# Layer 1's input stage: the silu of a strip moved into the next strip's convolution, and its normalised input made one strip earlier

## The chip, the cores and the metric

The kernel runs on one core of a Trainium2 chip, in float32. The time is the device time of one execution in microseconds (us), from three runs. A core has engines that run side by side and in order, each through its own queue: TensorE (PE; its weight loads are listed as PEld), VectorE (DVE), ScalarE (ACT), GpSimd (POOL), and SyncE (SP), which here only issues DMAs. An engine that waits for a semaphore holds everything behind it in its queue.

## The reference

A batch of 8 images of 64 x 64 pixels with 192 channels goes through four layers, each of the form x + f(group norm of x). Layer 0 is a state-space block with convolutions and an MLP, layers 2 and 3 are 3 x 3 depthwise convolutions. The change lies in layer 1, a two-dimensional selective scan, and there in what comes ahead of the scan:

```
xz = einsum("bhwc,oc->bhwo", gn(x), in_proj_w)       # 192 -> 768
xa, z = split(xz, 2)                                 # 384 each
xc = depthwise_conv3x3(xa, conv_w) + conv_b
xc = silu(xc)
x_dbl = einsum("bkdl,kcd->bkcl", xs(xc), x_proj_weight)   # 4 directions, 44 rows each
...                                                  # scan over 4096 positions in 4 directions
```

`z` is made later, in the output stage of the layer.

## The kernel before

The program runs five stages one after the other: layer 0, the input stage of layer 1 (`layer1_in`), its scan, its output stage, and layers 2 and 3 together. The stages hand over through DRAM: `x1` comes from layer 0; `ur` (the silu's result, channels on partitions), `ut` (the same, positions on partitions) and `xd` (the projection for the scan) go to the scan.

`layer1_in` works in 64 strips: 8 images of 8 strips, a strip being 8 image rows, that is 512 positions (`NJ`). The 384 channels are 3 groups of 128 (index `o`). Three Python generators emit the instructions, and `together` takes a step of each in turn, in the order `turn`, `convolve`, `project`; a `yield` ends a step. The engines' queues hold exactly this order, as it is written out by hand (`every_engine`). A generator that has to wait yields until a count in `done` allows it to go on.

- `project` (L783 to L802), for strip q: `normed` (L734) issues the DMA of `xt` on SP and two ACT instructions (L739) that make the group-normed `g`. For each `o`, PE makes two matmuls `mm` (L793), and ACT copies the result into `xa` (L797), which has room for one image row above and one below. POOL then fills these border rows from the neighbouring strip (L799, L800).
- `convolve` (L804 to L835), for strip q: for each `o`, PE does the three vertical taps of the middle column as matmuls with diagonal matrices (`cv`, L815), ACT takes them out of PSUM with the bias (L817), and DVE adds the other six taps one by one (L823). After the third `o` one ACT instruction does silu on the whole of `u` (L832), and `done["conv"]` goes up. Because of the border row, convolution of strip q needs the projection of strip q+1; the projection emitted beside it is that of q+2.
- `turn` (L837 to L861), for strip q: SP sends `u` to `ur` (L843). For each of 4 blocks of 128 positions PE transposes `u` (three transposes, `tp`, L849) and projects it (three matmuls, `xp`, L852); I call this a pair. ACT copies the transposes into `uT` (L856), DVE copies the projections into `xdt` (L857). Then SP sends both away (L858, L859). `turn` begins when `done["conv"]` is at least q+2, so it is two strips behind the one being convolved.

The pools rotate: `u` and `xa` have four buffers, `xt`, `g` and `uT` two, and every PSUM tag (`mm`, `cv`, `tp`, `xp`) two banks.

The matmuls are float32. The trace lists each of them as two entries where 512 columns are moved, so an `mm` group (two matmuls) is four entries and a `cv` group (three) is six.

Of the kernel before, what the change touches and what calls it, by code (L numbers as in the profile page):

```python
# [10 lines left out]
AF = mybir.ActivationFunctionType  # L11
# [22 lines left out]
def mk(pool, shape, tag, **kw):  # L34
    Names.n += 1
    return pool.tile(shape, F32, tag=tag, name=f"{tag}_{Names.n}", **kw)
# [44 lines left out]
def make_diag(nc, pool, w, nct, ident, tag, plus_one=False):  # L81
    P = w.shape[0]
    dg = mk(pool, [P, nct, 3, P], tag)
    for ct in range(nct):
        for j in range(3):
            s = w[:, ct, 3 * j + 1 : 3 * j + 2]
            if j == 1 and plus_one:
                nc.vector.scalar_tensor_tensor(dg[:, ct, j, :], ident[:P, :P], s, ident[:P, :P], ALU.mult, ALU.add)
            else:
                nc.vector.tensor_scalar(dg[:, ct, j, :], ident[:P, :P], s, None, ALU.mult)  # L90
    return dg
# [55 lines left out]
def together(*threads, beside=()):  # L147

    threads = list(threads)
    while threads:  # L150
        for t in list(threads) + list(beside):
            if next(t, threads) is threads and t in threads:
                threads.remove(t)


def every_engine(tc):
    ET = mybir.EngineType
    return tc.manual_schedule(engines={ET.PE, ET.DVE, ET.Activation, ET.Pool})
# [595 lines left out]
@with_exitstack  # L754
def layer1_in(ctx: ExitStack, tc, a, load, w_in, normed, ur, ut, xd, cst):

    nc = tc.nc
    ident = cst[0]
    wp = ctx.enter_context(tc.tile_pool(name="wi1", bufs=1))
    cw, cb = load("conv_w", [DP, DT, 9]), load("conv_b", [DP, DT])  # L760
    w_xp = load("w_xp", [DP, DT, K1 * XC])
    dg = make_diag(nc, wp, cw, DT, ident, "dg")
    sb = ctx.enter_context(tc.tile_pool(name="si1", bufs=2))
    psum = ctx.enter_context(tc.tile_pool(name="pi1", bufs=2, space=PSUM))
    xdt = [mk(wp, [128, NJ // 128, K1, 1 + XC], f"xdt{i}") for i in range(2)]
    for t in xdt:
        nc.vector.memset(t, 1.0)
    R = NJ // W
    strips = [(b, r) for b in range(B) for r in range(NCH)]
    rows, us = {}, {}  # L770
    done = {"in": 0, "conv": 0, "out": 0}

    def xa_rows(q):

        if q not in rows:
            t = rows[q] = mk(sb, [DP, DT, (R + 2) * W], "xa", bufs=4)
            if strips[q][1] == 0:
                nc.gpsimd.memset(t[:, :, 0:W], 0.0)
            if strips[q][1] == NCH - 1:
                nc.gpsimd.memset(t[:, :, (R + 1) * W :], 0.0)  # L780
        return rows[q]

    def project():  # L783
        for q, (b, r) in enumerate(strips):
            while done["conv"] < q - 2:
                yield
            _, g = normed(sb, b, r)
            yield
            t = xa_rows(q)
            for o in range(DT):  # L790
                ps = mk(psum, [128, NJ], "mm")
                for ct in range(CT):
                    nc.tensor.matmul(  # L793
                        ps, w_in[:, ct, o * 128 : (o + 1) * 128], g[:, ct, :], start=ct == 0, stop=ct == CT - 1
                    )
                yield
                nc.scalar.copy(t[:, o, W : W + NJ], ps)  # L797
            if r > 0:
                nc.gpsimd.tensor_copy(t[:, :, 0:W], rows[q - 1][:, :, NJ : NJ + W])  # L799
                nc.gpsimd.tensor_copy(rows[q - 1][:, :, NJ + W :], t[:, :, W : 2 * W])  # L800
            done["in"] = q + 1
            yield  # L802

    def convolve():  # L804
        for q, (b, r) in enumerate(strips):
            while done["in"] < q + 1 + (r < NCH - 1) or done["out"] < q - 2:
                yield
            t = rows[q]
            u = us[q] = mk(sb, [DP, DT, NJ], "u", bufs=4)
            uv = u.rearrange("p d (h w) -> p d h w", w=W)  # L810
            tv = t.rearrange("p d (h w) -> p d h w", w=W)
            for o in range(DT):
                ps = mk(psum, [128, NJ], "cv")
                for dy in range(3):
                    nc.tensor.matmul(ps, dg[:, o, dy, :], t[:, o, dy * W : dy * W + NJ], start=dy == 0, stop=dy == 2)  # L815
                yield
                nc.scalar.activation(u[:, o, :], ps, AF.Identity, bias=cb[:, o : o + 1])  # L817
                yield
                for dy in range(3):
                    for dx in (-1, 1):  # L820
                        w0, w1 = max(0, -dx), W - max(0, dx)
                        tap = 3 * dy + dx + 1
                        nc.vector.scalar_tensor_tensor(  # L823
                            uv[:, o, :, w0:w1],
                            tv[:, o, dy : dy + R, w0 + dx : w1 + dx],
                            cw[:, o, tap : tap + 1],
                            uv[:, o, :, w0:w1],
                            ALU.mult,
                            ALU.add,
                        )  # L830
            yield
            nc.scalar.activation(u, u, AF.Silu)  # L832
            del rows[q]
            done["conv"] = q + 1
            yield  # L835

    def turn():  # L837
        for q, (b, r) in enumerate(strips):
            while done["conv"] < min(q + 2, len(strips)):
                yield  # L840
            u = us.pop(q)
            t0 = r * NJ
            nc.sync.dma_start(ur[b][:, :, t0 : t0 + NJ], u)  # L843
            uT = mk(sb, [128, NJ // 128, DIN], "uT")
            xt = xdt[q % 2]
            for i in range(NJ // 128):
                ps = mk(psum, [128, NJ], "tp")
                for o in range(DT):
                    nc.tensor.transpose(ps[:, o * 128 : (o + 1) * 128], u[:, o, i * 128 : (i + 1) * 128], ident)  # L849
                px = mk(psum, [128, NJ], "xp")  # L850
                for o in range(DT):
                    nc.tensor.matmul(  # L852
                        px[:, 0 : K1 * XC], u[:, o, i * 128 : (i + 1) * 128], w_xp[:, o, :], start=o == 0, stop=o == 2
                    )
                yield
                nc.scalar.copy(uT[:, i, :], ps[:, 0:DIN])  # L856
                nc.vector.tensor_copy(xt[:, i, :, 1:], px[:, 0 : K1 * XC].rearrange("p (k c) -> p k c", k=K1))  # L857
            nc.sync.dma_start(ut[b][t0 : t0 + NJ, :].rearrange("(t q) d -> q t d", q=128), uT)  # L858
            nc.sync.dma_start(xd[b][t0 : t0 + NJ].rearrange("(t q) k c -> q t k c", q=128), xt)  # L859
            done["out"] = q + 1  # L860
            yield  # L861

    with every_engine(tc):
        together(turn(), convolve(), project())
# [447 lines left out]
```

## Time and profile before

| | us |
|---|---|
| median of 3 runs | 26510.6 |
| lowest and highest run | 26507.2, 26526.69 |
| the profiled execution | 26508.04 |
| its span, first to last instruction | 26506.2 |
| layer 0 | 0 to about 5745 |
| input stage of layer 1 | about 5745 to 7435 |
| scan of layer 1 | about 7435 to 23690 |
| output stage of layer 1 | about 23690 to 24960 |
| layers 2 and 3 | about 24960 to 26506 |

The scan takes 16255 of the 26506 us; of it nothing is touched. The stage in question has 1690 us, 6.4% of the span. The mean granted TensorE clock over the whole run is 0.942 of full speed; in the input stage it is 0.87, in the scan 1.00.

How a line is read: a group's line names the line of the kernel, the engine, the operation and the tiles (written <- read), then the total busy time, the mean duration of one in ns, and after the second bar the idle time of the engine just ahead of these instructions with what ended it. In a timeline, the first number is the start in us from the span's start, the second the duration; the bracket is the idle time before and what ended it. A line of stretches gives for each engine the busy time, with the number of instructions in brackets, in the order PE, PEld, DVE, ACT, POOL, then the granted clock, the DMA engines' share and GB/s. Ends of matmuls are modelled, so lengths on PE are best taken from start to start.

### The profile page before, as it was taken

How to read it: one execution, taken by the hardware profiler on the slowest of the kernel's cores; microseconds unless marked ns; L12 is line 12 of the kernel's file. 1: busy time of each engine (PE TensorE's matmuls, PEld its weight loads, DVE VectorE, ACT ScalarE, POOL GpSimd, SP SyncE). 2: the span in 40 equal slices, each digit the busy share in tenths (PEclk: the TensorE clock that was granted, in tenths of full speed). 3: DMA queues.
4: the chain of work that ended last, by engine and by line, in shares of the span. 5: the costliest groups of instructions: out<-in, count | busy, mean ns of one | idle time of the engine just before them, and what ended most of it. 6: DMA issues, size and time to landing. Idle time of an engine off the chain costs nothing.

```text
span 26506.2 us, 442347 instructions
## 1 busy us (share of the span) xinstructions
PE 23817.3 (90%) x156160; PEld 18514.6 (70%) x156160; DVE 22196.4 (84%) x25001; ACT 20110.0 (76%) x40019; POOL 17618.6 (66%) x18396
## 2 busy tenths in 40 slices
PE   7888888887799999999999999999999999987766
PEld 4444444444478888888888888888888888863322
DVE  6777777655589999999999999999999999986566
ACT  4555555433379999999999999999999999984322
POOL 2222222210079999999999999999999999972100
PEclk8888888888899999999999999999999999998878
DMA  1111111112233333333333333333333333346411
GB/s 55 42 43 43 42 43 42 34 44 89 90 103 97 94 102 96 95 101 96 96 100 98 94 101 97 96 99 98 95 99 99 95 98 97 96 137 198 126 34 29
DMA packets 1461962, 2275.55 MB, mean 86 GB/s; under 512 B 247181, under 2 KB 773133, under 8 KB 1458202
## 3 DMA queue, kind: packets, MB, share of 16 engines
q1 hardware_dynamic: 1445402, 2196.90, 28.2%
q0 software_dynamic: 14336, 50.34, 0.5%
q8 instruction: 1232, 20.19, 0.3%
q14 instruction: 992, 8.13, 0.1%
HBM read 1811.37 MB, written 435.42 MB: 85 GB/s over the span
## 4 chain that ended last, share of the span: by engine, by line
PE 36%; ACT 29%; DVE 13%; POOL 13%; issue 6%; DMA 2%; POOLq 0%; SPq 0%; DVEq 0%; ACTq 0%
ACT dA L1039 12%; POOL hc L1089 10%; PE pd L1045 6%; ACT sb L1023 6%; PE yt L978 5%; DVE h L1080 5%; ACT bd L1023 4%; PE y L643 3%; PE fc L677 3%; DVE x L71 2%; DVE u L823 2%; PE mm L793 2%; DMA yin<-y 2%; PE pd L1047 2%; PE mm L399 2%
## 5 line engine op out<-in xcount | busy, mean ns | idle before, releaser
L1089 POOL TENSOR_TENSOR hc<-h,bc 128x512 f32<-128x512 f32 x12288 | 15425.9, 1289 | 488.7 <-DVE h L1080 342.0
L1080 DVE TENSOR_TENSOR_SCAN h<-dA,st,pd 128x512 f32<-128x512 f32 x10752 | 12949.9, 1263 | 530.9 <-PE pd L1045 369.4
L1039 ACT ACTIVATE dA<-dl,A_logs 128x512 f32<-128x512 f32 x12288 | 8787.0, 715 | 46.9 <-DVE h L1080 39.6
L978 PE MATMUL yt<-sq,hc 128*128 128x128 f32 x49152 | 7488.5, 275 | 198.8 <-POOL hc L1089 97.3
L1045 PE MATMUL pd<-bd,dut 128*128 128x128 f32 x49152 | 6582.1, 277 | 254.4 <-DVE h L1080 232.1
L1045 PEld LDWEIGHTS pd<-bd,dut 128*128 128x128 f32 x49152 | 5969.2, 192 | 610.3 <-PE yt L978 343.0
L978 PEld LDWEIGHTS yt<-sq,hc 128*128 128x128 f32 x49152 | 5668.1, 141 | 642.1 <-POOL hc L1089 623.3
L1023 ACT ACTIVATE sb<-dut,xt 128x384 f32<-128x384 f32 x8192 | 4763.5, 606 | 1.1 <-DVE dut L964 1.0
L1047 PE MATMUL pd<-sq,sb 128*128 128x128 f32 x24576 | 3739.5, 275 | 9.1 <-DVE h L1080 0.2
L1047 PEld LDWEIGHTS pd<-sq,sb 128*128 128x128 f32 x24576 | 2820.9, 141 | 480.6 <-DVE dl L951 380.8
L1023 ACT ACTIVATE bd<-sq,xt 128x128 f32<-128x128 f32 x8192 | 3011.1, 393 | 0.0
L1080 DVE TENSOR_TENSOR_SCAN h<-dA,pd 128x512 f32<-128x512 f32 x1536 | 1772.6, 1204 | 114.8 <-PE pd L1045 75.6
L71 DVE SCALAR_TENSOR_TENSOR x<-x,w,x 96x3969 f32<-96x3969 f32 (+1 forms) x192 | 838.3, 4366 | 488.6 <-ACT x L64 485.6
L538 POOL TENSOR_TENSOR xdt<-xb,dtv 128x384 f32<-128x384 f32 x256 | 220.7, 862 | 1365.5 <-ACT xb L532 1365.5
L800 POOL COPY xa<-xa 128x192 f32<-128x192 f32 x56 | 19.9, 356 | 1387.9 <-ACT xa L797 1387.9
L413 POOL COPY halo<-raw 128x12 f32<-128x12 f32 x64 | 12.8, 201 | 1380.8 <-ACT raw L403 1380.8
L304 DVE SCALAR_TENSOR_TENSOR x<-xs,cpe_w,x 96x504 f32<-96x504 f32 (+1 forms) x1024 | 899.4, 878 | 30.2 <-ACT x L292 20.4
L823 DVE SCALAR_TENSOR_TENSOR u<-xa,conv_w,u 128x504 f32<-128x504 f32 x1152 | 850.1, 743 | 63.5 <-ACT u L817 25.1
L937 PE MATMUL mm<-xs,w_dt 13*128 13x512 f32 x1536 | 863.0, 641 | 1.8 <-DVE dl L951 1.0
L677 PE MATMUL fc<-ff,fc_w 128*96 128x512 f32 x1536 | 858.9, 676 | 2.7 <-DVE xo L680 2.7
L1091 POOL COPY st<-h 128x3 f32<-128x3 f32 x4096 | 821.8, 201 | 0.0
L793 PE MATMUL mm<-g,w_in 96*128 96x512 f32 x768 | 487.5, 769 | 333.4 <-ACT g L739 332.9
(234 smaller groups left out, 26955.9 us busy)
## 6 DMA issues: line engine op xcount, KB each, us to landing
bc<-bcd SPq DMA_DIRECT2D x4096, 256.0 KB
yin<-y SPq DMA_DIRECT2D x256, 768.0 KB
csb<-csd SPq DMA_DIRECT2D x256, 384.0 KB
dut<-ut SPq DMA_DIRECT2D x128, 768.0 KB
y<-ys SPq DMA_DIRECT2D x128, 768.0 KB
dut<-ut SPq DMA_DIRECT2D x256, 384.0 KB
y<-ys SPq DMA_DIRECT2D x256, 384.0 KB
xt<-x1d SPq DMA_DIRECT2D x128, 384.0 KB
```

Of the source, the lines that this page charges most:

```text
L71: nc.vector.scalar_tensor_tensor(d[:, h0:h1, w0:w1], s[:, h0 + dy : h1 + dy, w0 + dx : w1 + dx], w[:, ct, tap : tap + 1], d[:, h0:h1, w0:w ...
L304: nc.vector.scalar_tensor_tensor(d[:, :, w0:w1], s[:, dy : dy + R, w0 + dx : w1 + dx], w[:, ct, tap : tap + 1], d[:, :, w0:w1], ALU.mult, ...
L677: nc.tensor.matmul(ps, f2w[:, o, ct * CP : (ct + 1) * CP], ff[:, o, :], start=o == 0, stop=o == 5)
L793: nc.tensor.matmul(ps, w_in[:, ct, o * 128 : (o + 1) * 128], g[:, ct, :], start=ct == 0, stop=ct == CT - 1)
L823: nc.vector.scalar_tensor_tensor(uv[:, o, :, w0:w1], tv[:, o, dy : dy + R, w0 + dx : w1 + dx], cw[:, o, tap : tap + 1], uv[:, o, :, w0:w1] ...
L978: nc.tensor.matmul(yt[:, t * 128 : (t + 1) * 128], src[:, t * 128 : (t + 1) * 128], mat, is_transpose=mat is ident, start=first and t == 0 ...
L1023: nc.scalar.activation(v, src, AF.Copy, scale=m["xt"][:, t, 1 + R1 + n : 2 + R1 + n])
L1039: nc.scalar.activation(dA, ready[s]["dl"][:, o, :], AF.Exp, scale=aneg[:, k, o, n : n + 1])
L1045: nc.tensor.matmul(dst, ready[s]["dut"][:, t, cols], brows[g, t], start=True, stop=True)
L1047: nc.tensor.transpose(dst, brows[g, t][:, cols], ident)
L1080: nc.vector.tensor_tensor_scan(h[:, o, rev], decay.pop(j)[:, rev], turned.pop(j)[:, rev], 0.0 if first else st[:, o, n : n + 1], ALU.mult, ...
L1089: nc.gpsimd.tensor_tensor(hc, h[:, o, :], held[g], ALU.mult)
```

## The change

```diff
     def project():
+        _, g = normed(sb, *strips[0])
         for q, (b, r) in enumerate(strips):
             while done["conv"] < q - 2:
                 yield
-            _, g = normed(sb, b, r)
-            yield
             t = xa_rows(q)
             for o in range(DT):
                 ps = mk(psum, [128, NJ], "mm")
...
                 yield
                 nc.scalar.copy(t[:, o, W : W + NJ], ps)
+            if q + 1 < len(strips):
+                _, g = normed(sb, *strips[q + 1])
             if r > 0:
...
                 yield
                 nc.scalar.activation(u[:, o, :], ps, AF.Identity, bias=cb[:, o : o + 1])
+                if o == 0 and q > 0:
+                    finish(q - 1)
                 yield
...
             yield
-            nc.scalar.activation(u, u, AF.Silu)
-            del rows[q]
-            done["conv"] = q + 1
-            yield
+        finish(len(strips) - 1)
+        yield
+
+    def finish(q):
+        nc.scalar.activation(us[q], us[q], AF.Silu)
+        del rows[q]
+        done["conv"] = q + 1
 
     def turn():
         for q, (b, r) in enumerate(strips):
-            while done["conv"] < min(q + 2, len(strips)):
+            while done["conv"] < q + 1:
                 yield
```

The silu of a strip is no longer issued at the end of its own convolution. `finish` issues it in the next strip's convolution, behind the first of that strip's three copies out of PSUM. `normed` for a strip is called at the end of the projection of the strip before, behind the third copy into `xa`, so its DMA and its two ACT instructions are emitted earlier; the step that it took for itself is gone. `turn` begins when its strip's silu is issued. The arithmetic, the tiles, the buffers and the number of instructions stay the same.

## The prediction

> **What bounds the kernel now.** I read the totals of the page first, then the stretches of the stages, then, inside the stretch of the input stage of layer 1, the groups, the waits, one strip of the timeline and the granted clock.
>
> ```profile
> PE 23817.3 (90%) x156160; PEld 18514.6 (70%) x156160; DVE 22196.4 (84%) x25001; ACT 20110.0 (76%) x40019; POOL 17618.6 (66%) x18396
> ...
> 5745.00:7435.00 1690.00, 1332.90 (x4247) 758.51 (x4246) 925.19 (x1479) 528.20 (x841) 40.74 (x128) 0.87 0.26 89
> ```
>
> The totals say little: they are an average over five stages. The second line is the stretch of the input stage (columns: length, then busy time of PE, PEld, DVE, ACT, POOL, granted clock, DMA share, GB/s): 1690 us, in which DVE works 925, ACT 528, and the DMA engines are busy 26%. PE shows 1333, but partly at a lowered clock. No engine is full, so the stage is a chain of waits. Its largest groups and waits:
>
> ```profile
> L823 DVE SCALAR_TENSOR_TENSOR u<-xa,conv_w,u 128x504 f32<-128x504 f32 x1152 | 850.1, 743 | 63.5 <-ACT u L817 25.1 <-DVE u L823 0.9
> ...
> L832 ACT ACTIVATE u<-u 128x1536 f32<-128x1536 f32 x64 | 94.9, 1482 | 394.0 <-DVE u L823 387.5 <-DVE xdt L857 6.5
> L857 DVE COPY xdt<-xp 128x176 f32<-128x176 f32 x256 | 86.3, 338 | 689.6 <-PE xp L852 689.6
> ...
> DVE xdt L857 <- PE xp L852: 689.6, 128, 8.3
> ACT u L832 <- DVE u L823: 387.5, 62, 6.3
> ...
> PE mm L793 <- ACT g L739: 332.9, 62, 6.4
> ```
>
> They form a ring: silu (L832) waits 6.3 us per strip for DVE's taps, PE waits 5.4 us for `g` (L739), which ACT issues behind that silu, and DVE waits for PE's projection `xp`. One strip shows it in order:
>
> ```profile
> 6414.68 1.48 ACT L832 ACTIVATE u<-u 128x1536 f32<-128x1536 f32 x1 [6.27 <-DVE u L823]
> 6416.07 1.50 ACT L739 ACTIVATE g<-xt,nbb,scb 96x512 f32<-96x512 f32 x2
> ...
> 6416.92 3.78 PE L793 MATMUL mm<-g,w_in 96*128 96x512 f32 x4 [5.44 <-ACT g L739]
> ...
> 6423.14 0.34 DVE L857 COPY xdt<-xp 128x176 f32<-128x176 f32 x1 [8.30 <-PE xp L852]
> ...
> 6428.74 1.88 PE L793 MATMUL mm<-g,w_in 96*128 96x512 f32 x4
> ...
> 6432.15 9.18 DVE L823 SCALAR_TENSOR_TENSOR u<-xa,conv_w,u 128x504 f32<-128x504 f32 x12
> ...
> 6441.42 1.48 ACT L832 ACTIVATE u<-u 128x1536 f32<-128x1536 f32 x1 [6.27 <-DVE u L823]
> ```
>
> From one silu to the next are 26.74 us here. From the first silu (5791.13) to the 62nd (7383.42), the last before two strips that have no more input projection, are 61 steps in 1592.3 us, 26.10 on average. The same four `mm` take 3.78 us after PE's pause and 1.88 later: the clock.
>
> ```profile
> 6436.90:6440.40 3.50, 1.32 (x4) 0.26 (x2) 3.36 (x5) 0.00 (x0) 0.00 (x0) 1.00 0.00 0
> 6440.40:6447.30 6.90, 3.64 (x5) 1.47 (x6) 1.14 (x3) 3.84 (x5) 0.00 (x0) 0.52 0.45 151
> 6447.30:6463.70 16.40, 16.27 (x63) 9.54 (x61) 11.19 (x18) 4.28 (x8) 0.64 (x2) 1.00 0.23 79
> 24640.93:24643.41 2.48, 0.45 (x1) 0.24 (x2) 1.76 (x1) 0.59 (x2) 2.06 (x1) 1.00 0.37 123
> 24643.88:24647.30 3.42, 3.42 (x5) 1.11 (x4) 1.07 (x1) 0.64 (x1) 2.31 (x1) 0.50 0.01 3
> 24469.14:24471.62 2.48, 0.06 (x1) 0.06 (x1) 1.76 (x1) 0.57 (x1) 0.00 (x0) 1.00 1.07 364
> 24471.62:24475.10 3.48, 3.48 (x9) 1.35 (x10) 0.00 (x0) 1.52 (x2) 3.19 (x1) 1.00 0.12 28
> ```
>
> The last column but two is the granted clock. A pause of 5.4 us halves it for 6.9 us. Pauses of 2.48 us, in the output stage, did it once (24643.88: 0.50) and not the other time (24471.62: 1.00). The trace's clock records change only at multiples of 3.41 us. Laying the pauses of about 2 to 4 us against that grid: with 1.98 us or more of pause inside one cell a full clock was always lowered for the next cell, with less the 2.48 us pauses never lowered it.
>
> [...] The trace has one such load (1283 ns) for 64 silus among Identity and Copy, so silu's new neighbours, of the same two kinds, cost no load.
>
> **The change part by part.** Per strip nothing is added or removed: 3 convolution groups, 3 input projections, 4 pairs of transpose and `xp`, 18 taps, 4 `xdt` copies, and the same DMAs. The orders change. Call the strip in convolution q. On PE, up to a rotation: cv0(q), mm0(q+2), pair 0 of q-1, cv1, mm1, pair 1, mm2, pair 2, cv2, pair 3. On ACT: cv0's copy, silu of q-1, the copies and transposes' copies, `g` of q+3 after the third `xa` copy. On DVE: taps 0, two `xdt` copies, taps 1, two copies, taps 2, and at once taps 0 of the next strip. `turn` now follows one strip behind, not two.
>
> *The waits removed.* `g` is made a strip ahead, so mm0 no longer waits for it: the 5.4 us of PE. Taps 0 of the next strip no longer stand behind `xp`: they run 4.6 us while silu runs.
>
> *The wait added.* Pair 0 of q-1 now needs silu of q-1, which needs taps 2. Behind that pair in PE's order stand cv1, mm1 and the rest of the strip, and DVE's second and fourth `xdt` copies wait for pairs 1 and 3. This makes the new ring. At full clock, from starts in the timeline: a convolution group 2.57 us (6426.17 to 6428.74), an `mm` group 1.72 (to 6430.46), a pair 1.23 (to 6431.69). The ring is
> silu 1.48; 0.15 to the first transpose (0.10 is seen from `g` to the weight load, 0.05 is my estimate); three pairs 3.69, cv1 and cv2 5.14, mm1 and mm2 3.44, and the fourth pair to its end 1.39 (6430.46 to 6431.85), together 13.66; 0.04 and 0.26 for `xdt`; six taps 4.59 (half of 9.18); 0.09 to silu. Sum 20.27 us.
> Beside it: pair 1 ends 8.5 us after silu's start, its copy and taps 1 end near 13.4, before pair 3 (15.3), so that branch has 1.6 us to spare. PE's own work is 3 x 2.57 + 3 x 1.72 + 4 x 1.23 = 17.79, DVE's 18 x 0.765 + 4 x 0.3 = 15, ACT's 8.7. So PE pauses 20.27 - 17.79 = 2.48 us in each strip, before pair 0.
>
> *The clock.* This pause lies just where the trace has both outcomes. By the grid, a pause of 2.48 lowers the clock when 1.98 us fall in one cell: 1.93 of 3.41 positions. A lowered cell costs half of 3.41, 1.7 us, on the ring. But the positions are not drawn at random: six cells are 20.48 us, so a strip of 20.27 moves the pause 0.21 earlier against the grid each time, until it enters the bad part, is delayed by up to 1.7 us, and leaves it again. The mean then settles at 20.48 (one lowered strip in eight). The kernel before does the same: its strips repeat 25.38, 26.32, 26.81, which are 23 cells. Bounds: never lowered 20.27, always lowered 21.97. I take 20.48.
>
> *Costed at nothing.* `xt` for `g` of q+3 is issued by SP behind the `ur` transfer, which waits for silu: about 2.3 us into the ring. In the trace both had landed 3.6 us after the issue of `xt` (6444.34 to about 6448), and ACT wants it only at about 10.8; cv2's copy behind it may be 2 us later still. Were it late, each us past that would be on the ring. The `ut` and `xd` transfers follow as before. `u` has four buffers, `xa` four, so one more strip held by silu frees them late by a copy only. POOL's halo copies (0.35 us) come after the third `xa` copy, about 4 us ahead of cv0 of the next strip.
>
> *Edges.* The last two strips without `mm`: 20.27 - 3.44 = 16.8, plus 1.7 for a pause of over 4 us, 18.5 each, against 18.41 and 18.09: +0.5. The tail holds four pairs after the last silu, not six: -2.5. In the beginning mm1 stands ahead of cv1: +0.3.
>
> *The sum.* 61 x (26.10 - 20.48) = 343; with the edges 345 us less. The profiled execution took 26508.0 us (span 26506.2 and 1.8 around it): 26163. The median of the runs is 2.6 us above it: 26166, rounded 26165. The scan behind starts on the last `xd` transfer, so all of the gain moves its start.
>
> **The rivals.**
> *The pause lowers the clock in half of the strips or more.* For it: 1.93 of 3.41 positions; against it: the locking just told, which needs the sum right within 0.2 us below 20.48. Strips of 21.2 to 21.97: at 21.97, 61 x 4.13 = 252, with edges 254: 26257.
> *PE becomes the bound.* If PE got past the waiting pair, 17.79 us a strip: 61 x 8.31 = 507, 26002. Against it: cv1 stands behind pair 0 in PE's order. A part of it holds if my waits are too long: 19.5 gives 61 x 6.6 = 403, 26106.
> *Another wait takes the ring's place*, at 25.3 to 27 us a strip, and nothing can be told from no change: for it speaks only that three engines in order share short buffers (two PSUM banks each); against it, each bank's reader ends over 1 us before its next writer.
> *Slower, by the clock.* After its pause PE starts with transposes and 176-column matmuls; [...] the clock stays at half through the strip. From 13.66 at full clock the ring's PE part becomes 27.3, the strip 33.9: 61 x 7.8 = 476 more, 26985. It decides from 5.8 us of extra PE time on, that is four lowered cells in a row. Against it: at 7426.7 to 7431 the kernel before runs only such pairs, and from the fourth on they are 1.23 us apart again.
>
> **How the numbers follow.** Locked near 20.1 to 20.8: 0.65, range 26140 to 26190. Half or more of the strips lowered: 0.17. Below 20.1 a strip: 0.11. No change: 0.03. Slower: 0.02. Gains between the second case and no change: 0.02. The range 26125 to 26260 takes in the second case's bound and, on the low side, strips of 19.8 us, 0.5 less than the ring's sum. 0.2% is 53 us, about what a measurement here can tell from none; all cases but two are faster by more: faster 0.95, same 0.03, slower 0.02.
>
> **What would show it.** In the profile after: silu to silu about 20.5 us; PE waiting some 2.5 us a strip for silu, now ahead of the transposes and not ahead of `mm`; no wait for `g`; DVE's wait for `xp` down from 11 us a strip to about 5 (3.4 and 1.6); one strip in eight with a half-clock cell; clock of the stage near 0.97. I am wrong if `g` waits for `xt`, if the clock of the stage stays at 0.9, or if the taps wait for cv's copy.

## The result, and the profile after

The changed kernel takes 26176.6 us (median of 4 runs, 26172.0 to 26178.8) against 26512.9 for the kernel before (4 runs): ratio 0.9871, 95% interval 0.9856 to 0.9887, or 336 us less. 26165 had been forecast. The profiled execution of the changed kernel took 26178.8 us, its span is 26177.0.

Where the 329 us between the two spans lie, from the first `g` and the last issue of an `xd` transfer in each trace: the input stage went from 1680.9 to 1340.6 us, 340.3 less. What stands ahead of it took 6.6 us more in this execution, and what comes behind it 19078.4 in place of 19073.9 us. Neither is touched by the change; in the nine profiled executions of this study the stage begins between 5751 and 5761 us, and the part behind it takes between 19066 and 19083 us.

Two stretches of the changed kernel (columns as before: length, PE, PEld, DVE, ACT, POOL, granted clock, DMA share, GB/s), the whole stage and its steady part:

```profile
5745.00:7100.00 1355.00, 1186.31 (x4259) 687.90 (x4257) 928.41 (x1496) 531.67 (x844) 64.37 (x129) 0.97 0.33 112
5800.00:7000.00 1200.00, 1068.51 (x3865) 617.65 (x3865) 832.80 (x1283) 478.39 (x760) 58.13 (x116) 0.98 0.33 114
```

DVE and ACT are busy about as long as before (928 and 532 us against 925 and 528), in a stretch that is 335 us shorter. PE's busy time fell from 1333 to 1186 us although it does the same matmuls: the clock of the stage went from 0.87 to 0.97. The groups of the stage, and its waits between 5800 and 7000 us (total, times, longest), that answer to those shown of before:

```profile
L826 DVE SCALAR_TENSOR_TENSOR u<-xa,conv_w,u 128x504 f32<-128x504 f32 x1152 | 850.0, 742 | 50.2 <-ACT u L818 12.5
...
L839 ACT ACTIVATE u<-u 128x1536 f32<-128x1536 f32 x64 | 94.9, 1483 | 112.1 <-DVE u L826 112.0
L863 DVE COPY xdt<-xp 128x176 f32<-128x176 f32 x256 | 86.3, 338 | 363.0 <-PE xp L858 363.0
```

```profile
DVE xdt L863 <- PE xp L858: 332.9, 118, 6.9
PEld tp L855 <- ACT u L839: 179.5, 58, 3.4
...
PE tp L855 <- ACT u L839: 131.5, 58, 2.5
ACT u L839 <- DVE u L826: 100.0, 58, 2.0
```

Silu's idle time fell from 394 to 112 us and DVE's wait for `xp` from 690 to 363, which is 5.7 us a strip where about 5 had been forecast. In the steady part PE's wait for `g` is gone; in its place PE waits for silu, 2.27 us a strip, ahead of the transposes. One strip of the changed kernel in order:

```profile
6416.24 1.48 ACT L839 ACTIVATE u<-u 128x1536 f32<-128x1536 f32 x1 [2.00 <-DVE u L826]
...
6417.78 0.55 PE L855 MATMUL tp<-sq,u 128*128 128x128 f32 x3 [2.54 <-ACT u L839]
...
6419.06 2.74 PE L816 MATMUL cv<-xa,dg 128*128 128x512 f32 x6
...
6424.78 0.34 DVE L863 COPY xdt<-xp 128x176 f32<-128x176 f32 x1 [4.11 <-PE xp L858]
6425.04 4.63 DVE L826 SCALAR_TENSOR_TENSOR u<-xa,conv_w,u 128x504 f32<-128x504 f32 x6
...
6426.98 1.52 ACT L739 ACTIVATE g<-xt,nbb,scb 96x512 f32<-96x512 f32 x2
...
6428.52 0.55 SPq L736 DMA_DIRECT2D xt<-x1d  x1
...
6431.52 0.34 DVE L863 COPY xdt<-xp 128x176 f32<-128x176 f32 x1 [1.61 <-PE xp L858]
6431.78 9.25 DVE L826 SCALAR_TENSOR_TENSOR u<-xa,conv_w,u 128x504 f32<-128x504 f32 x12
...
6436.51 1.48 ACT L839 ACTIVATE u<-u 128x1536 f32<-128x1536 f32 x1 [1.72 <-DVE u L826]
```

Silu to silu are 20.27 us (PE's 2.54 and silu's 2.00 ahead are of a strip of 20.55; 2.26 and 1.72 are usual). This is the ring of the forecast, with all its links: silu, pairs on PE, the fourth `xdt` copy (its wait of 1.61 us is the last to end), six taps, silu. Of the 63 steps 49 take 20.26 or 20.27 us. Nine take 21.58 to 21.69, about every seventh. A stretch around one of these shows why:

```profile
6478.60:6482.00 3.40, 3.40 (x14) 2.21 (x15) 3.04 (x5) 0.87 (x2) 0.00 (x0) 1.00 0.61 231
6496.70:6498.40 1.70, 0.00 (x0) 0.00 (x0) 1.66 (x3) 1.10 (x1) 0.00 (x0) 0.99 0.00 0
6498.40:6501.80 3.40, 2.96 (x10) 2.80 (x11) 3.19 (x6) 1.34 (x3) 0.00 (x0) 0.50 0.52 196
6501.80:6518.00 16.20, 16.20 (x57) 8.85 (x55) 9.08 (x16) 5.76 (x10) 1.17 (x2) 1.00 0.30 100
```

The first line follows a pause of 2.26 us and runs at full clock; the second lies inside another pause of 2.26 us, and the 3.4 us behind it run at half clock (0.50, the third number from the end), with 10 matmuls in place of 14.

### The profile page after: what moved, and what is told of

It reads as the page before. It is cut to its first block, busy times and chain, and to the rows that moved or that the text cites. A ratio compares the mean times of both kernels' runs of the same rounds, so it can differ in the third digit from the quotient of the medians.

```text
span 26177.0 us, 442405 instructions
## 1 busy us (share of the span) xinstructions
PE 23676.9 (90%) x156160; PEld 18442.5 (70%) x156160; DVE 22201.3 (85%) x25001; ACT 20110.8 (77%) x40019; POOL 17658.9 (67%) x18396
## 4 chain that ended last, share of the span: by engine, by line
PE 37%; ACT 29%; POOL 13%; DVE 13%; issue 6%; DMA 2%; POOLq 0%; SPq 0%; DVEq 0%; ACTq 0%
ACT dA L1045 12%; POOL hc L1095 10%; PE pd L1051 6%; ACT sb L1029 6%; PE yt L984 5%; DVE h L1086 5%; ACT bd L1029 4%; PE y L643 3%; PE fc L677 3%; DVE x L71 2%; PE pd L1053 2%; DMA yin<-y 2%; PE mm L399 2%; PE mm L943 2%; PE y L576 1%
## 5 line engine op out<-in xcount | busy, mean ns | idle before, releaser
L304 DVE SCALAR_TENSOR_TENSOR xs<-x0h,cpe_w,xs 96x504 f32<-96x504 f32 (+1 forms) x1024 | 757.8, 745 | 23.7 <-ACT xs L292 2.5
L643 PE MATMUL y<-hn,fc_w 96*128 96x512 f32 x1536 | 750.2, 627 | 0.1
```

Source lines behind the costliest of these rows:

```text
L304: nc.vector.scalar_tensor_tensor(d[:, :, w0:w1], s[:, dy : dy + R, w0 + dx : w1 + dx], w[:, ct, tap : tap + 1], d[:, :, w0:w1], ALU.mult, ...
L643: nc.tensor.matmul(ps, f1w[:, ct, o * 128 : (o + 1) * 128], hn2[q][:, ct, :], start=ct == 0, stop=ct == CT - 1)
```

## The experiments

Seven kernels were run, each compared with the kernel before on the same chip. The theory is the forecast's: the step of a strip is a ring through the engines' queues, and PE's pause in it decides on the clock. The rivals are named with each.

**The change in parts.** The change does three things: `g` a strip ahead, silu behind the next strip's first bias copy, and `turn` one strip behind in place of two.

`g` a strip ahead and nothing else:

```diff
     def project():
+        _, g = normed(sb, *strips[0])
         for q, (b, r) in enumerate(strips):
...
-            _, g = normed(sb, b, r)
-            yield
...
+            if q + 1 < len(strips):
+                _, g = normed(sb, *strips[q + 1])
             if r > 0:
```

> The kernel before with only the input normalised a strip ahead; silu and turn as they were. By the ring theory PE no longer waits for g, and silu (1.48), two copies and the bias copy stand between one strip's taps and the next: a step of about 18.6 us, 26065 us, faster than the changed kernel. If moving silu is what the gain comes from, PE stands behind silu as before: 24 to 26 us a step, 26400 to 26510.

Measured: 26066.6 us (26044.4 to 26074.9), ratio 0.9831, interval 0.9816 to 0.9845. The steps are 18.59 us. So this part alone gains 444 us, more than the whole change. What PE still waits for (5900 to 6800 us, 49 strips), and the timeline from one silu to the next taps:

```profile
PE mm L792 <- ACT xa L796: 26.7, 49, 0.8
...
6406.27 1.48 ACT L833 ACTIVATE u<-u 128x1536 f32<-128x1536 f32 x1 [6.27 <-DVE u L824]
6407.66 0.57 ACT L796 COPY xa<-mm 128x512 f32<-128x512 f32 x1
...
6408.13 0.48 ACT L857 COPY uT<-tp 128x384 f32<-128x384 f32 x1
...
6408.50 0.70 ACT L818 ACTIVATE u<-cv,conv_b 128x512 f32<-128x512 f32 x1
...
6409.24 4.70 DVE L824 SCALAR_TENSOR_TENSOR u<-xa,conv_w,u 128x504 f32<-128x504 f32 x6 [1.11 <-ACT u L818]
```

Silu still waits 6.27 us, and what stands behind it now costs PE little: in place of `g` it is the first `xa` copy, for which `mm` waits 0.5 us a strip (26.7 us in 49 waits). Between two strips' taps lie silu, two copies and the bias copy, about 3 us, in which DVE does only two `xdt` copies.

The change without that part, so silu and `turn` as changed and `g` made in its old place:

```diff
     def project():
-        _, g = normed(sb, *strips[0])
         for q, (b, r) in enumerate(strips):
...
+            _, g = normed(sb, b, r)
+            yield
...
-            if q + 1 < len(strips):
-                _, g = normed(sb, *strips[q + 1])
```

> The changed kernel with the normalised input made in its old place; silu and turn as changed. The first input projection moves behind the second convolution group, so the ring holds three of them, not two: 20.27 + 1.72 = 21.99 us, and PE's pause of 4.2 us lowers the clock in every strip, 1.7 us more: about 23.7 us a step, 26375 us. If moving silu alone carries the gain: near 26176.

Measured: 26366.9 us (26365.0 to 26369.9), ratio 0.9946, interval 0.9931 to 0.9960. The steps are 23.6 us on average. Most are 23.67 to 23.68 with a lowered clock; the four without come to 21.98 or 21.99, the full-clock ring of the expectation, and seven with two lowered cells in a row take about 24.4. PE pauses 3.98 us a strip ahead of the transposes:

```profile
6411.16 1.51 ACT L739 ACTIVATE g<-xt,nbb,scb 96x512 f32<-96x512 f32 x2
...
6411.31 0.55 PE L854 MATMUL tp<-sq,u 128*128 128x128 f32 x3 [3.98 <-ACT u L838]
```

The change without its third part, `turn` two strips behind as it was:

```diff
     def turn():
         for q, (b, r) in enumerate(strips):
-            while done["conv"] < q + 1:
+            while done["conv"] < min(q + 2, len(strips)):
```

> The changed kernel with one line put back: turn again begins when two more strips have had their silu, so PE's transposes never wait for the silu just issued. If the ring silu - pairs - xdt - taps sets the changed kernel's step of 20.3 to 20.5 us, PE has nothing to wait for, the clock stays full and PE's own 17.8 us set the step: about 26010 us. If something else sets it (DVE's taps, PSUM banks, transfers), the step stays near 20.5 and the time near 26176.

Measured: 26000.4 us (25992.3 to 26002.6), ratio 0.9806, interval 0.9790 to 0.9822. The steps are 17.79 us, to the hundredth the sum of PE's own work in the forecast. Its steady stretch:

```profile
5900.00:6800.00 900.00, 900.00 (x3344) 526.94 (x3343) 723.64 (x1115) 411.03 (x659) 51.28 (x102) 1.00 0.38 131
```

PE is busy for the whole 900 us at full clock: it has no wait left. The third part of the change is thus what made the new ring, and it costs 2.7 us a strip: 26176.6 - 26000.4 = 176 us. Silu's new place, on the other hand, is worth something once `g` is ahead and `turn` two strips behind: the step is 17.79 us with it and 18.59 without it, 26066.6 - 26000.4 = 66 us. Silu's place alone, with `g` and `turn` as they were, was not run.

**The clock.** In the kernel before, five matmuls that wait for nothing were put into PE's pause; their results are overwritten by the projection that follows.

```diff
                 ps = mk(psum, [128, NJ], "mm")
+                for _ in range(5 if o == 0 else 0):
+                    nc.tensor.matmul(ps, w_in[:, 0, 0:128], w_in[:, 1, 0:NJ], start=True, stop=True)
                 for ct in range(CT):
```

> The kernel before with five more matmuls a strip (their results are overwritten), put into PE's pause ahead of the first input projection; they wait for nothing. By the clock theory the pause falls from 5.6 to 1.3 us, the clock stays full and the step falls from 26.1 to 23.4 us, so about 26345 us though work is added: of the change's gain about half is then clock and half waits. If the clock only follows and costs nothing, the time stays at 26513 or rises.

Measured: 26363.9 us (26356.5 to 26375.3), ratio 0.9945, interval 0.9930 to 0.9959: with 4.3 us of matmuls more in each strip, 147 us less. After the first, all steps but one (23.78) are 23.48 or 23.49 us up to the last two, and the clock of the steady stretch is full:

```profile
5900.00:6800.00 900.00, 856.36 (x2919) 468.62 (x2918) 548.19 (x844) 310.50 (x499) 23.15 (x75) 1.00 0.29 100
```

It is 19 us above what was expected. 11 of these come ahead of the first silu, which stands 50.9 us behind the first `g` in place of 39.7: three strips are projected there, and PE's pauses there come to only 1.9 us in the kernel before, where the added matmuls take 12.9. So of the 5.55 us that the change takes off a step (26.10 to 20.55) the clock alone is worth about 2.6 in the kernel before.

The same in the changed kernel, with one matmul made twice ahead of its shorter pause:

```diff
                 ps = mk(psum, [128, NJ], "mm")
+                for _ in range(1 if o == 0 else 0):
+                    nc.tensor.matmul(ps, w_in[:, 0, 0:128], g[:, 0, :], start=True, stop=True)
                 for ct in range(CT):
```

> The changed kernel with the first matmul of each strip's first input projection made twice (0.86 us more of PE work a strip, overwritten), just ahead of PE's pause. By the theory that a pause of more than 2 us in one cell of 3.41 us lowers the clock, the pause of 2.3 us falls to 1.4, no strip is lowered any more, every step is 20.27 us, and the time falls by 61 x 0.21 = 13 us to about 26163. If the 21.6 us strips have another cause, they stay, one in six or seven, and the time stays at 26176; if PE bounds the strip, 0.86 x 61 = 52 us more.

Measured: 26160.4 us (26145.6 to 26162.6), ratio 0.9869, interval 0.9852 to 0.9885. As a time this is not apart from the changed kernel's (0.9871). The steps decide: from the second on, up to the last two, all are 20.26 or 20.27 but one of 20.55, none is 21.6, and the clock records have no lowered cell between 5801 and 7035 us. The 21.6 us steps were the clock.

**Silu's place on the ring.** Silu in three instructions, two of them earlier:

```diff
                 if o == 0 and q > 0:
                     finish(q - 1)
+                if o > 0:
+                    nc.scalar.activation(u[:, o - 1, :], u[:, o - 1, :], AF.Silu)
                 yield
...
     def finish(q):
-        nc.scalar.activation(us[q], us[q], AF.Silu)
+        nc.scalar.activation(us[q][:, DT - 1, :], us[q][:, DT - 1, :], AF.Silu)
```

> The changed kernel with silu in three instructions of 512: the first two groups' right after the bias copy of the next group, only the third where the whole silu was. By the ring theory some 0.6 us of silu are left on the ring in place of 1.48: a step of 19.4 us, with a pause too short for the clock, so about 26176 - 61 x 1.1 = 26110 us, though ACT has more instructions. If silu is not on the ring: 26176 or slightly more.

Measured: 26088.7 us (26080.9 to 26094.1), ratio 0.9843, interval 0.9828 to 0.9857. The steps are 19.19 or 19.20 us. Silu is on the ring; 0.2 us more than expected came off, because two of the first block's three transposes no longer wait for the last part of silu:

```profile
6407.38 0.38 PE L857 MATMUL tp<-sq,u 128*128 128x128 f32 x2
6408.27 0.63 ACT L841 ACTIVATE u<-u 128x512 f32<-128x512 f32 x1 [1.72 <-DVE u L828]
...
6408.95 0.33 PE L857 MATMUL tp<-sq,u 128*128 128x128 f32 x1 [1.19 <-ACT u L841]
```

**A faster version.** On the kernel with `turn` two strips behind, where PE has no wait left, one tap of the first channel group was moved from PE to DVE:

```diff
-                for dy in range(3):
-                    nc.tensor.matmul(ps, dg[:, o, dy, :], t[:, o, dy * W : dy * W + NJ], start=dy == 0, stop=dy == 2)
+                on_pe = 2 if o == 0 else 3
+                for dy in range(on_pe):
+                    nc.tensor.matmul(ps, dg[:, o, dy, :], t[:, o, dy * W : dy * W + NJ], start=dy == 0, stop=dy == on_pe - 1)
...
-                    for dx in (-1, 1):
+                    for dx in (-1, 1) if dy < on_pe else (-1, 0, 1):
```

> The kernel with turn two strips behind (26000 us), and in the first of the three channel groups one of the middle column's taps moved from PE (0.86 us) to DVE (one more instruction of 0.76). If PE alone sets its step of 17.79 us, the step falls to 16.93 us and DVE's 16.0 still fit: about 25948 us. If ACT, banks or transfers set it, the step stays at 17.8.

Measured: 25941.2 us (25940.3 to 25944.9), ratio 0.9788, interval 0.9773 to 0.9802. The steps are 16.92 or 16.93 us. PE was the only bound at 17.79, and this is the fastest kernel of the study: 567 us less than its kernel before, 235 less than the changed one.

The steps beside each other (mean of the 61 steps from the first silu to the 62nd):

| kernel | step, us | PE's longest wait in a steady strip, us | median, us |
|---|---|---|---|
| before | 26.10 | 5.4 | 26512.9 |
| before, pause filled | 23.44 | 1.1 | 26363.9 |
| silu and `turn` moved, `g` not | 23.64 | 4.0 | 26366.9 |
| changed | 20.55 | 2.3 | 26176.6 |
| changed, pause shortened | 20.30 | 1.4 | 26160.4 |
| changed, silu in parts | 19.20 | 1.2 | 26088.7 |
| `g` alone | 18.61 | 0.5 | 26066.6 |
| `g` and silu, `turn` two behind | 17.69 | none | 26000.4 |
| the same, one tap on DVE | 16.85 | none | 25941.2 |

The last two means are below the steady steps of 17.79 and 16.93 us because the first two steps of these kernels are shorter.

## Why the prediction was right

- *The ring and its sum, 20.27 us.* The mechanism held, and 49 of 63 steps are 20.26 or 20.27. That it held to the hundredth is luck: in the strip shown above, silu's start to the first transpose is 1.54 us (1.63 in the sum), from there to the fourth `xdt` copy 13.74 (13.70), that copy to the taps 0.26 (0.26), the taps to silu 4.73 (4.68), and the differences cancel. The experiments changed three of its terms and moved the step as the sum says, within 0.2 us: one `mm` group more (21.98 to 21.99 without the clock's part, 21.99 expected), silu shortened (19.2, 19.4 expected), the wait of the pairs for silu taken away (17.79).
- *PE's own work, 17.79 us a strip*, given as the bound of a rival: it is the step of the kernel that has no such wait. That rival failed for the changed kernel for the reason given, that cv1 stands behind the waiting pair.
- *The clock settles the mean at 20.48.* From the third silu to the 62nd, 59 steps average 20.48 us. One step in seven is longer, by about 1.35 us, where one in eight by up to 1.7 had been expected. The kernel with the shortened pause shows that nothing else lengthens them. Six cells of 3.413 us are 20.48, as was argued. The figure behind it held less widely than the forecast said: in the output stage of before, 1.98 us of pause in a cell lowered the clock, and here 1.60 us did in some cells (last section). The pause of 2.26 us is longer than either, so the argument did not hang on it.
- *The pause: 2.48 forecast, 2.26 in most strips by the profile.* The profile's wait is counted from the modelled end of the last `mm` group, 1.88 us behind its start, where the next matmul would have started after 1.72; and the pair behind the pause takes 1.28 us from start to start in place of 1.23 (6417.78 to 6419.06). With these 0.16 and 0.05 the pause is 2.47.
- *The edges.* First `g` to first silu: 39.73 before, 39.97 after (+0.3 forecast). The tail from the last silu: 12.42 to 9.56 (-2.5 forecast). The last two steps: 36.50 to 37.67, 0.7 more than forecast.
- *What was missed: 4 us.* The first two steps take 23.19 and 21.85 us. The load of silu's table (ACT's `ACT_TABLE_LOAD`, 1283 ns, at 5796.68; the next such load is at 7109.33, behind the last silu) stands ahead of the first silu, so PE pauses 4.27 us there; the first step begins at half clock (0.50 for 6.83 us from 5798.64 on), and the second has a lowered cell as well (0.50 for 3.41 us from 5822.54 on). The stage gained 340.3 us, not 345. The parts outside it, which the change does not touch, took 11 us more in this profiled execution; the medians differ by 336.
- *A detail that was wrong.* `xt` was said to follow the `ur` transfer, to be issued about 2.3 us into the ring for the `g` of that strip. The timeline shows it at 6428.52, at the end of a `g`, whose buffer it fills; with two buffers it serves the `g` two strips later. No `g` waits for `xt` in the steady part, so the cost of nothing stands, with far more to spare than was said.
- *The split of the gain* was not forecast: filling the pause alone gives 147 us, `g` alone 444, and the parts do not add up, as each moves the same few waits.

The slower case, a clock that stays at half through the strip, did not come: behind the lowered cell at 6498.40 the next 16.2 us run at 1.00.

## What to carry to other kernels

When engines work in order, list for each step which instruction waits and what stands behind it in its queue, and add up the ring that closes; here the sum from start-to-start times of the old trace gave the steady step to 0.1%. A stage that consumes what another engine has just finished can be worth another strip of distance where buffers allow it: the same move with `turn` two strips behind (510 us less than the kernel before) or `g` ahead alone (444) beats the whole change (336). A pause of PE was worth filling here: in the kernel before it was 5.4 us long and the clock was half (0.52) for 6.9 us around its end, and with 4.3 us of matmuls in it, whose results are not used, the kernel takes 147 us less.

## What the runs showed that was not expected

The 1.98 us of pause in a 3.41 us cell, read off the output stage of before, is not what it took in the changed kernel. In its steady part ten cells lowered the clock of the next. All ten end in the pause, of which 1.600 to 2.11 us lie in them, with `mm` ahead of it; such cells with up to 1.596 us did not. Cells that begin with the pause, with transposes behind it, never did, and they reach 1.77 us. Two pairs of a cell and the next, the first of the changed kernel, the second of the one with silu and `turn` moved and `g` not:

```profile
7006.97:7010.38 3.41, 1.82 (x5) 0.51 (x3) 3.27 (x6) 1.55 (x2) 0.00 (x0) 1.00 0.51 162
7010.38:7013.79 3.41, 2.74 (x10) 2.74 (x11) 3.20 (x5) 1.57 (x3) 0.00 (x0) 0.50 0.46 174
...
6405.76:6409.17 3.41, 1.57 (x4) 0.38 (x2) 3.23 (x6) 0.69 (x1) 0.00 (x0) 1.00 0.90 308
6409.18:6412.58 3.40, 1.27 (x9) 1.27 (x10) 3.29 (x5) 2.81 (x4) 0.00 (x0) 1.00 0.05 11
```

In the first pair PE is busy for 1.82 us with `mm` and the next cell is lowered (0.50). In the second it is busy for only 1.57 us, with `cv`, and the next cell keeps the full clock (1.00). In that kernel transposes follow the pause as well, but `cv` stands ahead of it, and no cell with up to 1.98 us of pause lowered the clock, while all from 2.06 us on did. So it is not the transposes behind the pause that made 1.60 us enough. What PE does ahead of it differs: the timeline has `mm` on 96 rows (96*128) and `cv` on 128 (128*128). The kernel before has `cv` ahead of its pause too, and `mm` behind it: between 5800 and 7350 us its cells that end in the pause kept the full clock with up to 2.00 us of it, and lost it from 2.09 us on. Whether the rows make the difference was not tried.
